# Norm scales computed in place: one product with the mean matrix, then logarithm and exponential

## The chip, the cores and the metric

The kernel runs on one core of a Trainium2 chip. The metric is the device time of one execution in microseconds (us). Before the change it is 3188.66 us, the median of three runs from 3187.61 to 3190.03.

The engines of the core work side by side, each through its own queue in order. In the profile PE is TensorE's products and PEld its weight loads, DVE is VectorE, ACT is ScalarE, POOL is GpSimd and SP the engine that issues most DMAs.

## What is computed

Four layers, one after the other, on a residual of 4 sequences of 1024 tokens with 128 channels, all in fp32. Each layer is a half FFN, an attention and a half FFN again, each behind a layer norm without weights:

```python
def _layernorm(x, axis=-1, eps=1e-05):
    m = jnp.mean(x, axis=axis, keepdims=True)
    v = jnp.var(x, axis=axis, keepdims=True)
    return (x - m) / jnp.sqrt(v + eps)
...
x = x + 0.5 * ffn(_layernorm(x))
x = x + attn(_layernorm(x))
x = x + 0.5 * ffn(_layernorm(x))
```

The FFN of layers 0 and 2 is a mixture of 8 experts (top 2, hidden size 512; gelu in layer 0, relu in layer 2). The FFN of layer 1 is dense with silu and hidden size 384. In layer 3 the FFN mixes each token with the one before it. Attention is: in layer 0, over the 16 heads within a token; in layer 1, softmax attention with rotary positions; in layer 2, a linear attention with decay; in layer 3, a recurrence over tokens, whose output goes through a norm over each head's 8 channels (a group norm) before it is gated and projected.

## The kernel before

**Layout.** The residual stays in SBUF, one tile of 128 channels x 1024 tokens for each sequence: channels lie on partitions and tokens along the free dimension. Work goes mostly in halves of 512 tokens, which fill one PSUM bank. A mean or a variance over channels is therefore a sum over partitions[...]. Constants for it are in the pack `c0`: `center` (identity minus 1/128, so that a product with it takes the mean off), `mean` (all 1/128), `ident` (identity). The pack `c3` has `gcenter` and `gmean` for the groups of layer 3.

**A norm.** It appears in five places with the same steps: `l1_ffn` (line 597, a whole sequence, from then on in two halves), `prepare` in `l1_attn` (line 671, a whole sequence), `l2_half` (line 861), `normed` (line 936, called by layer 3's FFN and by `l3_prepare`), and `l3_finish` (line 1133, the group norm). The steps, for four tiles of 128 tokens in a half:

1. one product with `center` into a bank; ScalarE squares it to SBUF, and a copy of it (`xc`) is made by ScalarE or VectorE;
2. for each tile of 128 tokens, a product with the squares as weights and one column of `mean` as moving operand; it gives the tokens' variances with tokens on partitions, one column for each tile;
3. ScalarE takes the root with the small constant added, VectorE the reciprocal, both on 4 or 8 columns (the function `scales`, line 262, does steps 2 and 3 for `l1_ffn`, `l2_half` and for layer 0's attention);
4. for each tile, a product of that column, broadcast to 128 columns as weights, with `ident`; it brings the scales back to tokens along the free dimension, the same on all partitions, in a bank;
5. VectorE multiplies `xc` by the bank.

In `l3_finish` step 2 has 16 columns of `gmean`, and between 3 and 4 ScalarE copies the 16 scales of each token to 128 columns (`wide`).

The routers of layers 0 and 2 and layer 0's attention have norms of their own kind, with tokens on partitions.

**Order.** The layers' tasks are Python generators. `lanes` (line 1197) interleaves several of them by the costs that each `yield` states; in layer 0 the dense FFNs of layer 1 stand beside the last experts, in layer 2 they stand at the start, and the attention halves stand beside experts; in layer 3 five lanes run: the recurrence, two with the starts and two with the ends of a sequence. A scheduler then orders each engine's instructions, and puts in the waits. In layer 1's attention TensorE's order is as written by hand: its main loop has steps of scores and values, and `prepare` for the next sequence advances by one `yield` with each step.

Nearly all products are issued by the helper `mm`, so that they carry its line, 227, in the profile. An fp32 product is two passes, and so two instructions of PE and of PEld. Where a function of ScalarE isn't in the table set that is loaded, the build puts a table load (ACT_TABLE_LOAD) ahead of it.

Of the kernel before, what the change touches and what calls it, by code (L numbers as in the profile page):

```python
# [12 lines left out]
AF = mybir.ActivationFunctionType  # L13
# [3 lines left out]
P = 128  # L17
# [42 lines left out]
def _constants():  # L60

    p = np.arange(P)
    f = np.float32
    n8, n16 = np.arange(8), np.arange(16)
    t = np.arange(P)

    c0 = [
        ("ident", np.eye(P, dtype=f)),
        ("mean", np.full((P, P), 1.0 / P, f)),
        ("rev", np.broadcast_to((8 - n8).astype(f), (P, 8))),  # L70
        ("below", (p[:, None] < p[None, :]).astype(f)),
        ("ones", np.ones((P, P), f)),
        ("lane", np.broadcast_to(p.astype(f), (P, P))),
        ("column", np.broadcast_to(np.arange(BLOCKS, dtype=f), (P, BLOCKS))),
        ("full", np.broadcast_to((SLOTS * np.arange(GT)).astype(f), (P, GT))),
        ("center", np.eye(P, dtype=f) - f(1.0 / P)),
        ("token", (1.0 + p[:, None] + P * np.arange(2 * GT)).astype(f)),
        *[
            (f"spare{g}", (1.0 + 2 * g * NT * P + p[:, None] + P * np.arange(blocks_of(g * NT))).astype(f))
            for g in range(1, GROUP + 1)  # L80
        ],
    ]

    dd = p % HD
    freqs = np.power(f(10000.0), -np.arange(0, HD, 2, dtype=f) / f(HD)).astype(f)
    angles = (np.arange(S, dtype=f)[:, None] * freqs).astype(f)
    sin, cos = np.sin(angles).astype(f), np.cos(angles).astype(f)
    sign = np.where(dd < HD // 2, -1.0, 1.0).astype(f)
    c1 = [
        ("cos", cos.T[dd // 2]),  # L90
        ("sin", sin.T[dd // 2] * sign[:, None]),
    ]

    n = np.maximum(t[None, :] - p[:, None], 0)
    bits = ((n[:, None, :] >> np.arange(7)[:, None]) & 1).astype(f)
    c2 = [("bit", bits), ("nobit", 1 - bits), ("causal", (t[None, :] >= p[:, None]).astype(f))]

    h, turned = p // HD, np.arange(2)[None, :, None]
    c3 = [
        ("sums", (h[:, None, None] == np.arange(32) - NH * turned).astype(f)),  # L100
        ("vrows", ((p % 32)[:, None, None] == NH * turned + h).astype(f)),
        ("bonus", (h[:, None] == p % NH).astype(f)),
        ("gcenter", np.eye(P, dtype=f) - (p[:, None] % NH == p % NH).astype(f) / HD),
        ("gmean", (p[:, None] % NH == n16).astype(f) / HD),
    ]
    return {"c0": c0, "c1": c1, "c2": c2, "c3": c3}

# [98 lines left out]
class Macaron:  # L206
# [55 lines left out]
    def scales(self, pool, wp, sq, tag, tiles=NT):  # L262

        var = self.t(pool, [P, tiles], "bank")
        for i in range(tiles):
            self.mm(var[:, i : i + 1], sq[:, i * P : (i + 1) * P], self.c0["mean"][:, 0:1])
        std = self.t(wp, [P, tiles], tag + "std")
        self.nc.scalar.activation(std, var, AF.Sqrt, bias=self.eps_ln)
        r = self.t(wp, [P, tiles], tag + "rstd")
        self.nc.vector.reciprocal(r, std)  # L270
        return r

# [322 lines left out]
    def l1_ffn(self, ps, wp, m, b):  # L597
        nc, c0 = self.nc, self.c0
        X = self.X[b]
        bank = lambda shape=(P, HALF): self.t(ps, list(shape), "bank")  # L600
        halves = [slice(h * HALF, (h + 1) * HALF) for h in range(2)]
        sq, xc = self.t(wp, [P, S], "sq", bufs=1), self.t(wp, [P, S], "xc", bufs=1)
        for c in halves:
            cen = bank()
            self.mm(cen, c0["center"], X[:, c])
            nc.scalar.activation(sq[:, c], cen, AF.Square)
            nc.vector.tensor_copy(xc[:, c], cen)
        r = self.scales(ps, wp, sq, "f")
        yield 4
        for hf, c in enumerate(halves):  # L610
            bc = bank((P, 4, P))
            for j in range(4):
                i = 4 * hf + j
                self.mm(bc[:, j, :], r[:, i : i + 1].to_broadcast([P, P]), c0["ident"])
            xn = self.t(wp, [P, HALF], "xn")
            nc.vector.tensor_tensor(xn, xc[:, c], bc.rearrange("p i t -> p (i t)"), ALU.mult)
            h = self.t(wp, [P, HIDC, HALF], "h", bufs=1)
            for i in range(HIDC):
                g = bank()
                self.mm(g, m["wg"][:, i, :], xn)  # L620
                s = self.t(wp, [P, HALF], "s")
                nc.scalar.activation(s, g, AF.Silu)
                u = bank()
                self.mm(u, m["wu"][:, i, :], xn)
                nc.vector.tensor_tensor(h[:, i, :], s, u, ALU.mult)
                yield 2
            o = bank()
            for i in range(HIDC):
                self.mm(o, m["wd"][:, i, :], h[:, i, :], start=i == 0, stop=i == HIDC - 1)
            self.add_half(b, c, o)  # L630
            yield 3
# [6 lines left out]
    def l1_attn(self, m, c1):  # L638
# [5 lines left out]
        with ExitStack() as ctx:  # L644
# [26 lines left out]
            def prepare(b):  # L671
# [5 lines left out]
                nc.scalar.copy(xc, cen)  # L677
                yield
                yield
                var = two((P, NT))  # L680
                for i in range(NT):
                    self.mm(var[:, i : i + 1], sq[:, i * P : (i + 1) * P], c["mean"][:, 0:1])
                std, r = self.t(self.lnp, [P, NT], "std"), self.t(self.lnp, [P, NT], "rstd")
                nc.scalar.activation(std, var, AF.Sqrt, bias=self.eps_ln)
                v.reciprocal(r, std)
                yield
                yield
                bc = two()
                for i in range(NT):
                    self.mm(bc[:, i * P : (i + 1) * P], r[:, i : i + 1].to_broadcast([P, P]), c["ident"])  # L690
                xn = self.t(self.lnp, [P, S], "xn")
                v.tensor_tensor(xn, xc, bc, ALU.mult)
                yield
                yield
                for w, wt, tag in ((m["wq"], m["wqt"], "qd"), (m["wk"], m["wkt"], "kd")):
# [165 lines left out]
    def l2_half(self, ps, wp, m, grow, X):  # L861
# [8 lines left out]
        q, qs = one("q", (P, 4, P)), one("qs", (P, 4, P))  # L870
        nc.scalar.activation(sq, cen, AF.Square)
        v.tensor_copy(xc, cen)
        r = self.scales(ps, wp, sq, "l", 4)
        bc = bank((P, 4, P))
        for j in range(4):
            self.mm(bc[:, j, :], r[:, j : j + 1].to_broadcast([P, P]), c0["ident"])
        v.tensor_tensor(xn, xc, bc.rearrange("p i t -> p (i t)"), ALU.mult)
        qp = bank()
        self.mm(qp, m["wq"], xn)
        nc.scalar.activation(q.rearrange("p c t -> p (c t)"), qp, AF.Relu, bias=m["bq"])  # L880
# [55 lines left out]
    def normed(self, ps, tmp, wp, b, h, before):  # L936

        nc, c0 = self.nc, self.c0
        x = self.X[b][:, h * HALF : (h + 1) * HALF]
        cen = self.t(ps, [P, HALF], "bank")  # L940
        self.mm(cen, c0["center"], x)
        sq, xc = self.t(tmp, [P, HALF], "n_sq"), self.t(tmp, [P, HALF], "n_xc")
        nc.scalar.activation(sq, cen, AF.Square)
        nc.scalar.copy(xc, cen)
        var = self.t(ps, [P, 4], "bank")
        for i in range(4):
            self.mm(var[:, i : i + 1], sq[:, i * P : (i + 1) * P], c0["mean"][:, 0:1])
        std, r = self.t(tmp, [P, 4], "n_std"), self.t(tmp, [P, 4], "n_r")
        nc.scalar.activation(std, var, AF.Sqrt, bias=self.eps_ln)
        nc.vector.reciprocal(r, std)  # L950
        bc = self.t(ps, [P, 4, P], "bank")
        for i in range(4):
            self.mm(bc[:, i, :], r[:, i : i + 1].to_broadcast([P, P]), c0["ident"])
        xn = self.t(wp, [P, HALF + 1], "xn", bufs=3)
        if before is None:
            nc.vector.memset(xn[:, 0:1], 0.0)
        else:
            nc.scalar.copy(xn[:, 0:1], before[:, HALF:])
        nc.vector.tensor_tensor(xn[:, 1:], xc, bc.rearrange("p i t -> p (i t)"), ALU.mult)
        return xn  # L960


# [170 lines left out]
    def l3_finish(self, ps, wp, m, c3, b, h, given):  # L1133
# [7 lines left out]
        sq, yc = self.t(wp, [P, HALF], "t1", bufs=1), self.t(wp, [P, HALF], "t2", bufs=1)  # L1141
        act(sq, cen, AF.Square)
        nc.scalar.copy(yc, cen)
        var = bank((P, 4, NH))
        for i in range(4):
            self.mm(var[:, i, :], sq[:, i * P : (i + 1) * P], c3["gmean"])
        std, rs = self.t(wp, [P, 4, NH], "gstd"), self.t(wp, [P, 4, NH], "grs")
        act(std, var, AF.Sqrt, bias=self.eps_gn)
        v.reciprocal(rs, std)
        wide = self.t(wp, [P, 4, HD, NH], "t3", bufs=1)  # L1150
        nc.scalar.copy(wide, rs.unsqueeze(2).to_broadcast([P, 4, HD, NH]))
        yield 5
        bc = bank((P, 4, P))
        for i in range(4):
            self.mm(bc[:, i, :], wide[:, i].rearrange("p j h -> p (j h)"), self.c0["ident"])
        v.tensor_tensor(yc, yc, bc.rearrange("p i t -> p (i t)"), ALU.mult)
        v.tensor_tensor(yc, yc, g, ALU.mult)
        o = bank()
        self.mm(o, m["olnb"], g, stop=False)
# [221 lines left out]
```

## Time and profile before

| | |
|---|---|
| median of the runs | 3188.66 us |
| the profiled execution | 3191.45 us |
| its span, first to last instruction | 3189.6 us |
| mean granted TensorE clock | 0.905 of full |
| instructions | 48448 |
| table loads, all of 1283 ns | 196 |
| LDWEIGHTS and MATMUL of `n_sq` (step 2 of `normed`) | 192 each |
| LDWEIGHTS and MATMUL of `n_r` (step 4 of `normed`) | 192 each |

A row of the page's groups has line, engine, operation, output and input with shapes, the count, busy time in us and the mean of one in ns, and then the idle time ahead of it with what ended it. In a timeline a row has start and duration in us. The chain that ended last is followed back from the last instruction to whatever released each step; its shares say which engine's work sets the end. The granted clock is the share of TensorE's full clock that the throttle let through.

### The profile page before, as it was taken

The numbers are of one execution on the slowest core, as the hardware profiler recorded it, in microseconds if no ns is written. First come the engines' busy times: TensorE is split into PE (matmuls) and PEld (weight loads), VectorE is DVE, ScalarE is ACT, GpSimd is POOL, SyncE is SP. The second block draws the span as 40 slices with busy tenths as digits, with TensorE's granted clock in tenths as the row PEclk, the third lists the DMA queues.
The fourth block names the chain that finished last, engine by engine and source line by source line (L and its number), as shares of the span: only waits on it lengthen the run. The fifth ranks groups of instructions, "written<-read, shape, count | busy, mean of one in ns | idle before, by whom it ended". The sixth has DMA issues, their size and how long they took to land.

```text
span 3189.6 us, 48448 instructions
## 1 busy us (share of the span) xinstructions
PE 2823.6 (89%) x18206; PEld 1677.6 (53%) x18206; DVE 1828.0 (57%) x3160; ACT 1633.3 (51%) x3633; POOL 794.8 (25%) x748
## 2 busy tenths in 40 slices
PE   7977548878969999999999999999998987899997
PEld 6856437666633333333333333579787985334333
DVE  3486967774226676676677774352565532355764
ACT  4655425656712565566556566455453544445342
POOL 3556306552440000000000000027543464000110
PEclk9988758888977999999999999989998997888997
DMA  6656315563500000000000000039555675000000
GB/s 218 217 169 203 115 51 169 166 196 105 159 15 9 6 6 5 6 5 6 20 5 6 3 1 1 9 115 297 191 182 164 205 260 167 0 0 0 7 7 13
DMA packets 122889, 277.63 MB, mean 87 GB/s; under 512 B 18016, under 2 KB 67296, under 8 KB 122528
## 3 DMA queue, kind: packets, MB, share of 16 engines
q1 hardware_dynamic: 101792, 231.77, 23.1%
q0 software_dynamic: 20864, 42.77, 4.5%
q8 instruction: 144, 2.36, 0.3%
q14 instruction: 89, 0.73, 0.1%
HBM read 238.43 MB, written 31.85 MB: 85 GB/s over the span
## 4 chain that ended last, share of the span: by engine, by line
PE 70%; DVE 8%; ACT 5%; DMA 3%; issue 2%; POOL 1%; ACTq 0%; SPq 0%; POOLq 0%; DVEq 0%
PE bank L227 36%; PE two L227 17%; PE o L227 8%; PE s L227 4%; DVE nm L729 2%; PE wave L1019 1%; ACT e_h L459 1%; DMA c_y<-res 1%; ACT L459 1%; DVE prod L554 1%; PE bank L449 1%; DMA e_xg<-rows,g_source 1%; DVE st L1117 1%; DVE o L556 1%; PE acc L1019 1%
## 5 line engine op out<-in xcount | busy, mean ns | idle before, releaser
L729 DVE TENSOR_REDUCE nm<-two 128x2 f32<-128x1024 f32 x512 | 626.8, 1225 | 287.8 <-PE s L227 268.4
L752 ACT ACTIVATE e<-s 128x512 f32<-128x512 f32 x1024 | 555.9, 594 | 405.7 <-PE s L227 402.7
L459 ACT ACTIVATE e_h<-bank,e_w 128x128 f32<-128x128 f32 x1304 | 449.5, 368 | 412.7 <-PE bank L227 378.3
L227 PE MATMUL s<-qm,kz 32*128 32x512 f32 x2048 | 633.7, 642 | 0.8 <-ACT e L752 0.8
L227 PE MATMUL bank<-e_x,e_w 128*128 128x128 f32 x2608 | 538.3, 309 | 85.9 <-ACT e_h L459 50.5
L227 PE MATMUL two<-kz,qz 32*128 32x512 f32 x2048 | 592.1, 663 | 21.5 <-DVE nm L729 2.7
L445 POOL DMA_INDIRECT e_xg<-rows,g_source x326 | 336.8, 1033 | 798.6 <-DVE g_target L412 353.5
L227 PEld LDWEIGHTS bank<-e_x,e_w 128*128 128x128 f32 x2608 | 410.0, 203 | 164.9 <-ACT e_h L459 94.0
L227 PE MATMUL bank<-e_w,e_h 128*128 128x128 f32 x2608 | 462.4, 293 | 18.4 <-ACT e_h L459 10.3
L471 POOL DMA_INDIRECT res<-e_y,g_target x326 | 358.9, 1101 | 282.4 <-DVE e_y L470 135.9
L227 PEld LDWEIGHTS bank<-e_w,e_h 128*128 128x128 f32 x2608 | 380.7, 202 | 40.1 <-ACT e_h L459 22.6
L227 PE MATMUL o<-e,va 128*32 128x256 f32 x4096 | 328.3, 392 | 0.1
L227 PEld LDWEIGHTS o<-e,va 128*32 128x32 f32 x4096 | 81.0, 108 | 389.6 <-issue 370.3
L227 PEld LDWEIGHTS two<-kz,qz 32*128 32x128 f32 x2048 | 159.4, 188 | 239.7 <-issue 163.6
L227 PEld LDWEIGHTS s<-qm,kz 32*128 32x128 f32 x2048 | 206.7, 183 | 11.4 <-issue 7.8
L470 DVE TENSOR_TENSOR e_y<-bank,e_w 128x128 f32<-128x128 f32 x326 | 93.9, 288 | 202.8 <-PE bank L227 189.3
L451 DVE COPY e_x<-bank 128x128 f32<-128x128 f32 x326 | 92.8, 285 | 189.7 <-PE bank L449 178.5
L717 POOL COPY va<-vd 128x256 f32<-128x256 f32 x16 | 6.7, 432 | 626.6 <-PE o L227 538.2
L1124 POOL TENSOR_TENSOR z<-st,r 128x512 f32<-128x512 f32 x32 | 46.2, 1443 | 416.8 <-DVE st L1117 333.3
L449 PE MATMUL bank<-c,e_xg 128*128 128x128 f32 x326 | 96.8, 298 | 34.0 <-DMA e_xg<-rows,g_source 31.0
L227 PE MATMUL bank<-g_cols,g_lanes 128*128 128x39 f32 (+1 forms) x512 | 83.4, 325 | 26.8 <-DVE g_cols L392 25.9
L227 PEld LDWEIGHTS bank<-g_cols,g_lanes 128*128 128x128 f32 x512 | 83.3, 251 | 30.3 <-issue 28.6
(300 smaller groups left out, 3683.2 us busy)
## 6 DMA issues: line engine op xcount, KB each, us to landing
e_w<-in_l0m_dram SPq DMA_DIRECT2D x170, 578.0 KB
e_w<-in_l2m_dram SPq DMA_DIRECT2D x156, 578.0 KB
c_y<-res SPq DMA_DIRECT2D x32, 512.0 KB
rows<-g_xt SPq DMA_DIRECT2D x16, 512.0 KB
e_xg<-rows,g_source POOLq DMA_INDIRECT x326
res<-e_y,g_target POOLq DMA_INDIRECT x326
x<-in_x_dram SPq DMA_DIRECT2D x4, 512.0 KB
qz<-qd SPq DMA_DIRECT2D x64, 32.0 KB
```

The costliest lines, as they stand in the source:

```text
L227: self.nc.tensor.matmul(out, lhsT, rhs, start=start, stop=stop)
L445: nc.gpsimd.indirect_dma_start(out=xg, out_offset=None, in_=rows[:, :], in_offset=at(source[:, k : k + 1]))
L449: nc.tensor.transpose(tp, xg, self.c0["ident"])
L451: nc.vector.tensor_copy(x, tp)
L459: nc.scalar.activation(h[:, fc, :], o[:, fc, :], func, bias=w[:, 2 * FC * P + fc : 2 * FC * P + fc + 1])
L470: nc.vector.tensor_tensor(y, o, w[:, MOE_W - D :], ALU.add)
L471: ins = nc.gpsimd.indirect_dma_start(out=res[:, :], out_offset=at(target[:, k : k + 1]), in_=y, in_offset=None)
L554: v.tensor_tensor(pv, ex.unsqueeze(2).to_broadcast(sh), values.unsqueeze(1).to_broadcast(sh), ALU.mult)
L729: v.tensor_reduce(nm[:, it, h, 2 * pair : 2 * pair + 2], s, AX.X, ALU.max, negate=True)
L752: nc.scalar.activation(es[g], s, AF.Exp, scale=scale)
L1019: i = self.nc.tensor.matmul(out, lhsT, rhs, start=start, stop=stop).ins
L1124: (pool if i else v).tensor_tensor(z, st[:, 0:HALF], r, ALU.mult)
```

## The change

Steps 2 to 4 are replaced in all five places. One product of the whole `mean` matrix (128 x 128) with the squares gives the variance of each token on all partitions at once, with tokens along the free dimension; for the groups, `gmean` is widened from 16 to 128 columns. ScalarE then computes the inverse root there, as exp(-0.5 ln(var + eps)), in two activations of the full width, the second over its own output in SBUF. VectorE's multiplication reads the result from SBUF instead of a bank.

```diff
-        ("gmean", (p[:, None] % NH == n16).astype(f) / HD),
+        ("gmean", (p[:, None] % NH == p % NH).astype(f) / HD),
...
+    def spread_scales(self, ps, sq, eps, mean=None):
+        var = self.t(ps, [P, HALF], "bank")
+        self.mm(var, self.c0["mean"] if mean is None else mean, sq)
+        self.nc.scalar.activation(sq, var, AF.Ln, bias=eps)
+        self.nc.scalar.activation(sq, sq, AF.Exp, scale=-0.5)
+        return sq
...
 l1_ffn
-        r = self.scales(ps, wp, sq, "f")
+        for c in halves:
+            self.spread_scales(ps, sq[:, c], self.eps_ln)
         yield 4
-        for hf, c in enumerate(halves):
-            bc = bank((P, 4, P))
-            for j in range(4):
-                i = 4 * hf + j
-                self.mm(bc[:, j, :], r[:, i : i + 1].to_broadcast([P, P]), c0["ident"])
+        for c in halves:
             xn = self.t(wp, [P, HALF], "xn")
-            nc.vector.tensor_tensor(xn, xc[:, c], bc.rearrange("p i t -> p (i t)"), ALU.mult)
+            nc.vector.tensor_tensor(xn, xc[:, c], sq[:, c], ALU.mult)
...
 prepare
-                var = two((P, NT))
-                for i in range(NT):
-                    self.mm(var[:, i : i + 1], sq[:, i * P : (i + 1) * P], c["mean"][:, 0:1])
-                std, r = self.t(self.lnp, [P, NT], "std"), self.t(self.lnp, [P, NT], "rstd")
-                nc.scalar.activation(std, var, AF.Sqrt, bias=self.eps_ln)
-                v.reciprocal(r, std)
+                nc.scalar.activation(sq, project(c["mean"], sq), AF.Ln, bias=self.eps_ln)
+                nc.scalar.activation(sq, sq, AF.Exp, scale=-0.5)
                 yield
                 yield
-                bc = two()
-                for i in range(NT):
-                    self.mm(bc[:, i * P : (i + 1) * P], r[:, i : i + 1].to_broadcast([P, P]), c["ident"])
                 xn = self.t(self.lnp, [P, S], "xn")
-                v.tensor_tensor(xn, xc, bc, ALU.mult)
+                v.tensor_tensor(xn, xc, sq, ALU.mult)
...
 l2_half
-        r = self.scales(ps, wp, sq, "l", 4)
-        bc = bank((P, 4, P))
-        for j in range(4):
-            self.mm(bc[:, j, :], r[:, j : j + 1].to_broadcast([P, P]), c0["ident"])
-        v.tensor_tensor(xn, xc, bc.rearrange("p i t -> p (i t)"), ALU.mult)
+        v.tensor_tensor(xn, xc, self.spread_scales(ps, sq, self.eps_ln), ALU.mult)
...
 normed
-        var = self.t(ps, [P, 4], "bank")
-        for i in range(4):
-            self.mm(var[:, i : i + 1], sq[:, i * P : (i + 1) * P], c0["mean"][:, 0:1])
-        std, r = self.t(tmp, [P, 4], "n_std"), self.t(tmp, [P, 4], "n_r")
-        nc.scalar.activation(std, var, AF.Sqrt, bias=self.eps_ln)
-        nc.vector.reciprocal(r, std)
-        bc = self.t(ps, [P, 4, P], "bank")
-        for i in range(4):
-            self.mm(bc[:, i, :], r[:, i : i + 1].to_broadcast([P, P]), c0["ident"])
+        self.spread_scales(ps, sq, self.eps_ln)
...
 l3_finish
-        var = bank((P, 4, NH))
-        for i in range(4):
-            self.mm(var[:, i, :], sq[:, i * P : (i + 1) * P], c3["gmean"])
-        std, rs = self.t(wp, [P, 4, NH], "gstd"), self.t(wp, [P, 4, NH], "grs")
-        act(std, var, AF.Sqrt, bias=self.eps_gn)
-        v.reciprocal(rs, std)
-        wide = self.t(wp, [P, 4, HD, NH], "t3", bufs=1)
-        nc.scalar.copy(wide, rs.unsqueeze(2).to_broadcast([P, 4, HD, NH]))
+        self.spread_scales(ps, sq, self.eps_gn, c3["gmean"])
         yield 5
-        bc = bank((P, 4, P))
-        for i in range(4):
-            self.mm(bc[:, i, :], wide[:, i].rearrange("p j h -> p (j h)"), self.c0["ident"])
-        v.tensor_tensor(yc, yc, bc.rearrange("p i t -> p (i t)"), ALU.mult)
+        v.tensor_tensor(yc, yc, sq, ALU.mult)
```

More of the change, by code (lines that the diff above doesn't have):

```diff
@@ L63, in _constants @@
     f = np.float32
-    n8, n16 = np.arange(8), np.arange(16)
+    n8 = np.arange(8)
     t = np.arange(P)
@@ L958, in normed @@
             nc.scalar.copy(xn[:, 0:1], before[:, HALF:])
-        nc.vector.tensor_tensor(xn[:, 1:], xc, bc.rearrange("p i t -> p (i t)"), ALU.mult)
+        nc.vector.tensor_tensor(xn[:, 1:], xc, sq, ALU.mult)
         return xn
```

## The prediction

> **What bounds the kernel now.** I read the page's engine shares first, then its chain that ended last, then busy time by stretch, and last the chain and the timeline inside a norm.
>
> ```profile
> PE 2823.6 (89%) x18206; PEld 1677.6 (53%) x18206; DVE 1828.0 (57%) x3160; ACT 1633.3 (51%) x3633; POOL 794.8 (25%) x748
> ...
> PE 70%; DVE 8%; ACT 5%; DMA 3%; issue 2%; POOL 1%; ACTq 0%; SPq 0%; POOLq 0%; DVEq 0%
> ```
>
> The chain that sets the end is TensorE's for 70% of the span, ScalarE's for 5%, although ScalarE is busy half the time. So a microsecond taken from TensorE is mostly a microsecond gained, and one added to ScalarE mostly isn't, until ScalarE's answers come later than TensorE's other work covers. By stretch (start:end, length, busy us of PE, PEld, DVE, ACT, POOL, granted clock, DMA share, GB/s):
>
> ```profile
> 0.00:715.00 715.00, 515.78 (x3096) 441.47 (x3097) 483.81 (x902) 378.45 (x972) 333.91 (x292) 0.83 0.53 167
> 715.00:915.00 200.00, 174.12 (x879) 123.60 (x878) 67.73 (x187) 125.17 (x240) 52.75 (x55) 0.89 0.37 113
> 915.00:2010.00 1095.00, 1053.62 (x8767) 378.77 (x8765) 702.61 (x686) 598.30 (x1088) 52.51 (x58) 0.97 0.03 6
> 2010.00:2260.00 250.00, 237.19 (x1342) 186.45 (x1341) 99.55 (x275) 120.80 (x344) 98.02 (x97) 0.92 0.49 159
> 2260.00:2490.00 230.00, 215.97 (x1492) 193.21 (x1492) 137.44 (x434) 105.04 (x305) 96.09 (x99) 0.93 0.54 172
> 2490.00:2690.00 200.00, 174.91 (x1301) 160.50 (x1299) 80.64 (x275) 100.87 (x322) 115.31 (x117) 0.94 0.73 236
> 2690.00:3190.00 500.00, 451.98 (x1336) 193.56 (x1336) 256.20 (x404) 204.71 (x364) 46.18 (x32) 0.85 0.01 5
> ```
>
> These are layer 0 up to its first dense FFN, its dense FFNs, layer 1's attention, layer 2 in three parts, layer 3. TensorE is at 87 to 96% wherever a changed norm runs. The first changed norm starts at about 717 us, so a quarter of the span can't move. Now one norm of layer 3 in the chain (start, us, what), where nothing lies beside it:
>
> ```profile
> 3149.41 0.61 ACT n_sq L943
> 3150.06 1.07 PE bank L227 x8
> 3151.15 0.27 ACT n_std L949
> 3151.44 0.19 DVE n_r L950
> 3151.68 1.17 PE bank L227 x8
> 3152.87 0.70 DVE xn L959
> ```
>
> From the end of the square to the multiplication: 2.85 us, of which TensorE works 2.24. The table load for the root isn't there: another root had left its table in place.
>
> **What the skill says.** "ScalarE: Activation LUTs", section "What ACT_TABLE_LOAD costs": about 1283 ns for a load plus about 1380 ns of drain at each change of set. The trace has the 1283 in every load, but no drain: at 3136.37 a load starts 0.02 us after the copy before it ends, and the root starts 0.02 us after the load. I use 1.28. The same page, "Table sets: the hidden batching unit", says that a logarithm followed by an exponential needs one load, there being a set with both. The changed kernel, built, stands otherwise: in its order of instructions a load precedes nearly every logarithm and another its exponential. The order decides. "TensorE: Matmul & The Clock Gate", section on the clock gate: idle stretches put TensorE at half clock. The trace agrees: a product of 512 columns shows 1.02 us at 3129.82 and after, and 1.92 us in the first lines below.
>
> **The change, part by part.** It was 32 half-sequence norms in layer 3 (24 `normed`, 8 group norms), 8 halves of `l2_half`, 16 halves of `l1_ffn`, and 4 whole-sequence norms in `prepare`.
>
> *Off TensorE.* Per half: 4 variance products with the squares as weights and 4 spreading products, each product two passes, so 8 and 8 instructions; on: one product of 512 columns, 2 passes. Occupancy at full clock: 0.97 and 0.97 us (weight loads of eight passes at 3150.05 and 3151.68) against 0.86 (2 x 0.43, the spacing of consecutive 512-column passes). Saved: 1.08 us. At half clock:
>
> ```profile
> 2697.66 1.86 PE L227 MATMUL bank<-c,n_sq 128*128 128x1 f32 x8 [0.69 <-ACT n_sq L943]
> ...
> 2700.18 2.04 PE L227 MATMUL bank<-c,n_r 128*128 128x128 f32 x8 [0.66 <-DVE n_r L950]
> ...
> 2702.02 1.92 PE L227 MATMUL bank<-x,c 128*128 128x512 f32 x2
> ```
>
> 1.78 + 1.78 - 1.71 = 1.85. With a half-clock share of (1 - clock)/0.5: layer 3 1.31 us x 32 = 42; layer 2 1.19 x 16 = 19; layer 0 1.25 x 8 = 10; `prepare` about 2.2 us each, three of them inside a full TensorE stream, 6.5. Sum 77 us. The built order agrees in count: 448 products fewer, 896 of 18206 rows.
>
> *On ScalarE.* Counting loads in the built orders: 196 before, 259 after: +9 in layer 0, 0 in layer 1 (there the root's load becomes the logarithm's), +28 in layer 2, +26 in layer 3. 63 x 1.28 = 81 us. Rows for the two functions:
>
> ```profile
> L883 ACT ACTIVATE k<-bank,l2a 128x512 f32<-128x512 f32 x8 | 5.5, 688 | 1.4 <-PE bank L227 1.4
> ...
> L994 ACT ACTIVATE t<-t 128x512 f32<-128x512 f32 x16 | 10.1, 629 | 0.5
> ```
>
> Logarithm 0.69 (from a bank, with a bias column), exponential 0.63 (from SBUF): 1.32 x 56 = 74; the four wide ones about 1.1 + 1.06 each, 9. Minus the roots (52 at 0.26 to 0.31, 14) and the wide copies (4.9). Sum +144 us, 51% to about 56%. VectorE loses only reciprocals of 0.2 to 0.5 us (12 us in all, under cover); its multiplication reads SBUF for PSUM at the same 0.69 (row of `qs`, 0.692).
>
> *The new wait.* From the end of the variance product to the normalised tile: 0.69 + 1.28 + 0.63 + 0.69 and four hand-offs of 0.03 to 0.05 = 3.45 us, all without TensorE. Behind it in ScalarE's order stand gelus, silus, tanhs and evictions of banks; TensorE, in order, waits for those. Before, the wait was in two pieces of about 0.6 and 0.75 us with products between. What hides it is TensorE's work placed between product and first use, read off the built order at full clock:
>
> - Layer 3: 19 of 24 norms have 3.4 us or more; five have 1.72, 2.58, 1.72, 0.86 and 0. Exposed there 10.4 us; the same places lost about 5.5 before: +5. The group norms' old path is as long as the new one (the last: variance products end at 3163.98, multiplication at 3168.04, with load, root, reciprocal, wide copy and products between, 4.06 us): 0. Further, 62 of ScalarE's 144 us lie here, on an engine 41% busy; bounds 0 and 31 (half of it late for TensorE), I take a quarter, +15. Layer 3: -42 + 5 + 15 = -22.
> - Layer 2, attention halves: 2.64 us of cover, with relus of the experts in the queue between and behind. 1.2 to 2 us exposed each, 1.5 x 8 = 12, against -9.5: +3.
> - Layer 2's dense FFNs: the first two sequences' four halves each take load, logarithm, load, exponential in turn (4 x 3.9 us) before the first silu; before, that silu came at 2022.08. It comes some 9 us later; two or three us of TensorE's work fill that. +7 and a little, against -9.5: about -1.
> - Layer 0's dense FFNs: -10, and 21 us more on a ScalarE that is 63% busy between gelus; half of it late: 0.
> - Layer 1: the load count is the same; the logarithm holds its bank for 0.85 us more than the root did, but TensorE waited for another bank then anyway (it stood from 1520.1 to 1521.0). -6.5 + 1.5 = -5.
>
> One bank fewer per norm is taken; that can only help. The queues of SP and POOL keep their instructions, with a few scatters and gathers in another place: 0, bounds -5 and +5.
>
> Sum: -22 + 3 - 1 + 0 - 5 = -25 us. The profiled execution took 3191.45 us (span 3189.6), 2.8 above the median of 3188.66; off the median that gives **3164 us**.
>
> **Rivals.**
>
> *A, the forecast:* TensorE's saving, a third kept. 0.48.
>
> *B, slower: table changes become the path.* Place: ScalarE's queue in layer 2 and 3, where each norm now holds it for 3.9 us (two loads, two functions) instead of 0.3 to 1.5, with expert activations and evictions behind. Price 144 us; it decides when over 77/144 = 54% of that is late for TensorE. At two thirds: -77 + 96 = +19, 3208 us. For: 63 more loads that a static order may not have made room for. Against: before, ScalarE's share of the chain was 5% of the span, a tenth of its busy time. 0.25.
>
> *C, all hidden:* -77, 3112 us. For: covers over 3.4 us in most places of layer 3. Against: layer 2's covers. 0.13.
>
> *D, nothing comes of it:* TensorE's shorter work is paid back as waits and, since it idles in longer pieces, as half clock; 3188 us. For: layer 3's clock is already 0.85 at 90% busy, and a single 3.45 us pause in place of two short ones can tip it. 0.14.
>
> **How the numbers follow.** A measurement of this kernel can tell about 0.2%, 6.4 us, from no change. A's own range is 3140 to 3180 (its 15 and 12 at their bounds). For 8 in 10 the range must go half into C and into B: 3125 to 3207. Faster: A 0.46, C 0.13, D 0.04: 0.63. Within: A 0.01, D 0.08, B 0.02: 0.11. Slower: the rest of B and D, A 0.01: 0.26.
>
> **What would show it.** Rows of PE 17310 and busy time down by some 70 us; ACT busy near 1777 us, 259 loads of 1283 ns; layer 3 shorter by about 20 us, layer 1 by 5, layer 2 and layer 0's end about even; in the tail a gap of about 3.4 us on TensorE between the variance product and the next. I am wrong if waits of PE for ACT's e_h or for evictions grow by more than 50 us in layers 2 and 3 (B), if layer 3's clock falls under 0.82 (D), or if no such gap appears anywhere (C).

## The result, and the profile after

The changed kernel takes 3216.22 us (median of 6 runs, 3209.14 to 3225.12), the kernel before, run beside it, 3189.09. The ratio is 1.009, 95% interval 1.0071 to 1.0108: 27 to 29 us slower, where 25 faster was forecast. The profiled execution has a span of 3207.2 us, against 3189.6; it is the fastest of the six, so the views below account for 17.6 us of the loss and not for all of the median's 27. First the engine shares of the kernel after:

```profile
PE 2764.0 (86%) x17310; PEld 1559.3 (49%) x17310; DVE 1822.5 (57%) x3108; ACT 1767.3 (55%) x3756; POOL 800.5 (25%) x748
```

TensorE's rows fell to 17310 and its busy time by 59.6 us; ScalarE's rose by 134.0. Both were foreseen. By stretch, the kernel after (columns as in the prediction's table; the cuts are at this run's own first changed norm, start of layer 1, and so on):

```profile
711.50:913.00 201.50, 165.52 (x761) 108.82 (x761) 67.01 (x183) 144.02 (x260) 54.60 (x56) 0.90 0.37 111
913.00:2008.00 1095.00, 1049.46 (x8647) 366.15 (x8646) 700.41 (x680) 605.27 (x1091) 51.45 (x57) 0.97 0.04 6
2008.00:2275.50 267.50, 236.01 (x1244) 175.87 (x1245) 102.17 (x280) 146.10 (x376) 99.53 (x99) 0.90 0.47 154
2275.50:2505.00 229.50, 204.02 (x1333) 176.59 (x1332) 129.57 (x407) 121.66 (x308) 91.83 (x94) 0.93 0.53 162
2505.00:2722.80 217.80, 185.15 (x1350) 165.22 (x1348) 87.06 (x300) 110.95 (x344) 118.15 (x119) 0.94 0.71 223
2722.80:3207.20 484.40, 412.63 (x878) 128.57 (x878) 251.63 (x355) 261.32 (x406) 48.97 (x32) 0.86 0.01 5
```

The same cuts in the kernel before, for layer 2's first part and layer 3:

```profile
2009.00:2262.00 253.00, 239.29 (x1352) 187.94 (x1352) 101.81 (x282) 122.93 (x351) 99.40 (x99) 0.92 0.49 160
2697.00:3189.60 492.60, 447.80 (x1326) 191.68 (x1326) 252.67 (x387) 202.26 (x356) 46.18 (x32) 0.86 0.01 5
```

Layer 3: TensorE's busy time fell from 447.8 to 412.6 us, but its idle time (length less busy) rose from 44.8 to 71.8. Layer 2's first part: busy 239.3 and 236.0, idle 13.7 and 31.5, at a clock of 0.90 for 0.92.

The table below cuts each profiled run at the first start of the same tiles (first square of the dense FFNs' norms, first square of `prepare`, last copy `os`, first and last square of `l2_half`, first `n_sq`, end), in us. The kernels of the experiments are in it too. "Start" is layer 0 before any changed norm; only before_joint and joint_all change something in it. Each row is one execution, and equal instructions vary: the other starts run from 712.8 to 721.9, layer 1 of mix and one_set takes 1081.3 and 1084.2, layer 3 of no_l1ffn and after 490.0 and 484.4. Differences of a few us in one cell prove little.

| run | start | layer 0, dense FFNs | layer 1 | layer 2, dense FFNs | attention | rest | layer 3 |
|---|---|---|---|---|---|---|---|
| before | 717.2 | 199.8 | 1091.4 | 255.3 | 217.1 | 216.2 | 492.6 |
| after | 712.8 | 201.9 | 1092.6 | 269.8 | 225.8 | 219.9 | 484.4 |
| one_set | 720.4 | 199.3 | 1084.2 | 254.3 | 212.6 | 218.7 | 460.0 |
| abs_rsqrt | 721.6 | 190.6 | 1086.8 | 253.4 | 212.3 | 218.6 | 465.9 |
| only_l3 | 717.6 | 200.9 | 1090.7 | 255.5 | 217.1 | 215.1 | 484.5 |
| no_l1ffn | 721.4 | 196.5 | 1095.2 | 256.2 | 225.7 | 217.7 | 490.0 |
| before_loads | 716.0 | 199.5 | 1093.7 | 251.3 | 220.8 | 216.3 | 512.2 |
| before_joint | 727.4 | 198.6 | 1087.0 | 252.8 | 217.9 | 217.2 | 485.1 |
| no_roots | 714.3 | 180.3 | 1087.1 | 253.7 | 213.1 | 217.4 | 462.6 |
| joint_all | 734.5 | 200.3 | 1081.2 | 256.7 | 212.4 | 216.3 | 460.8 |
| load_behind | 721.9 | 199.8 | 1086.9 | 264.6 | 227.8 | 220.5 | 475.3 |
| two_ahead | 719.6 | 202.1 | 1085.2 | 267.0 | 225.7 | 219.5 | 477.9 |
| mix | 720.9 | 189.7 | 1081.3 | 254.4 | 212.6 | 218.6 | 460.0 |

Before to after: -4 in the start, +2 and +1 in layer 0's dense FFNs and layer 1, +27 in layer 2, -8 in layer 3. The loss is made in layer 2, and layer 3's gain is a third of what was hoped.

What happens at layer 2's start is seen in stretches of 10 us, from the same point of the work (columns: stretch, length, busy us of PE, PEld, DVE, ACT, POOL, clock, DMA share, GB/s). Before:

```profile
2012.00:2022.00 10.00, 9.67 (x57) 6.87 (x56) 4.75 (x10) 5.30 (x8) 0.00 (x0) 1.00 0.20 64
2022.00:2032.00 10.00, 10.00 (x26) 4.39 (x25) 4.03 (x6) 3.58 (x6) 0.00 (x0) 1.00 0.00 0
```

and after:

```profile
2011.00:2021.00 10.00, 6.03 (x14) 2.32 (x12) 3.26 (x5) 8.39 (x10) 0.00 (x0) 0.88 0.20 64
2021.00:2031.00 10.00, 9.41 (x18) 3.59 (x17) 3.06 (x6) 9.85 (x12) 0.00 (x0) 0.77 0.00 0
...
2071.00:2081.00 10.00, 8.29 (x28) 4.13 (x27) 3.42 (x6) 9.70 (x23) 0.00 (x0) 1.00 0.00 1
```

ScalarE, 55% busy over the stage, is at 84 to 99% in these three (in the four left out it is at 34 to 62%), and TensorE idles 4 us in the first ten. The timeline of the kernel after shows what fills it (start, us, engine, instruction, and in brackets the engine's idle time before it and what ended it):

```profile
2013.40 1.28 ACT L278 ACT_TABLE_LOAD   x1 [1.30 <-PE bank L227]
...
2015.40 1.28 ACT L279 ACT_TABLE_LOAD   x1
2016.69 0.63 ACT L279 ACTIVATE sq<-sq 128x512 f32<-128x512 f32 x1
2017.34 1.28 ACT L278 ACT_TABLE_LOAD   x1
2018.63 0.69 ACT L278 ACTIVATE sq<-bank,eps_ln 128x512 f32<-128x512 f32 x1
2019.22 0.59 ACT L615 ACTIVATE sq<-bank 128x512 f32<-128x512 f32 x1
...
2019.86 2.08 PE L227 MATMUL bank<-sq,c 128*128 128x512 f32 x2 [3.97 <-ACT sq L615]
...
2029.49 0.60 ACT L628 ACTIVATE s<-bank 128x512 f32<-128x512 f32 x1
```

Loads for logarithm (L278) and exponential (L279) alternate; the second sequence's square stands behind three of them, and TensorE waits 3.97 us for it. The first silu starts at 2029.49. Before:

```profile
2022.08 0.60 ACT L622 ACTIVATE s<-bank 128x512 f32<-128x512 f32 x1 [0.82 <-PE bank L227]
```

Layer 2 begins at 2007.3 in the kernel after and at 2008.4 before (last copy `os`), so that the silu is 8.5 us late. The squares of the routings (L310 after) stand behind the next norms in the same queue, and the experts wait for the routings. SP's own queue, before and after:

```profile
2075.25 18.37 SPq L307 DMA_DIRECT2D rows<-g_xt  x2
2102.09 4.35 SPq L443 DMA_DIRECT2D e_w<-in_l2m_dram  x5
```

```profile
2085.23 14.38 SPq L316 DMA_DIRECT2D rows<-g_xt  x2
2112.90 3.81 SPq L452 DMA_DIRECT2D e_w<-in_l2m_dram  x5
```

Counted from the last copy `os`, the routed rows are written 11.1 us later and the first expert weights fetched 11.9 us later.

### The profile page after: what moved, and what is told of

It reads as the page before. It is cut to its first block, busy times and chain, and to the rows that moved or that the text cites. A ratio compares the mean times of both kernels' runs of the same rounds, so it can differ in the third digit from the quotient of the medians.

```text
span 3207.2 us, 46741 instructions
## 1 busy us (share of the span) xinstructions
PE 2764.0 (86%) x17310; PEld 1559.3 (49%) x17310; DVE 1822.5 (57%) x3108; ACT 1767.3 (55%) x3756; POOL 800.5 (25%) x748
## 5 line engine op out<-in xcount | busy, mean ns | idle before, releaser
L227 PE MATMUL bank<-e_x,e_w 128*128 128x128 f32 x2608 | 534.6, 308 | 100.0 <-ACT e_h L468 65.5
L227 PE MATMUL bank<-e_w,e_h 128*128 128x128 f32 x2608 | 457.6, 291 | 21.9 <-ACT e_h L468 13.7
L227 PEld LDWEIGHTS s<-qm,kz 32*128 32x128 f32 x2048 | 207.5, 183 | 13.8 <-issue 7.8
L479 DVE TENSOR_TENSOR e_y<-bank,e_w 128x128 f32<-128x128 f32 x326 | 93.8, 288 | 210.5 <-PE bank L227 198.6
```

Of the source, the lines that this page charges most:

```text
L227: self.nc.tensor.matmul(out, lhsT, rhs, start=start, stop=stop)
L479: nc.vector.tensor_tensor(y, o, w[:, MOE_W - D :], ALU.add)
```

## The experiments

Theories: **T1**, the 63 extra table changes on ScalarE cost the time. **T2**, the full-width functions and the long wait themselves. **T3**, the new static order of instructions. T4 to T6 came with the later runs.

**Loads taken out, nothing else moved (one_set).** After the instructions have been ordered, the load ahead of each logarithm is set by hand to the table set that holds both functions:

```diff
+    _one_set(nc)
...
+                if i.func == AF.Ln and not loaded:
+                    placed.append(mybir.InstLoadActFuncSet(
+                        name=nc.get_next_instruction_name(), engine=i.engine, debug=i.debug, ins=[], outs=[], act_func_set_id=6))
+                loaded = i.func == AF.Ln or (loaded and i.func == AF.Exp)
+            placed.append(i)
```

> The changed kernel with every order of instructions kept, but each logarithm's table load names the set that holds the exponential too, so the exponential needs none: 196 loads in place of 259 (layer 0 122, layer 1 1, layer 2 21, layer 3 52). T1 (the 63 extra table changes, standing in ScalarE's queue ahead of silus, routing and relus, are what cost the time): 3172 us, between 3160 and 3182; the first expert of layer 2 comes within 4 us of where it came before, instead of 12.6 later. T2 (the two full-width functions and the one long wait per norm are the cost; loads fall into idle time): 3210, between 3204 and 3216. T3 (the new static order, which puts routing and experts later, is the cost): as T2, and the first expert of layer 2 stays over 9 us late.

Measured: 3151.49 us, ratio to before 0.9879 (0.9859 to 0.9899). That beats both kernels, 38 us under before, and goes beyond T1's range. The first expert of layer 2 starts 123.5 us after layer 1's last `os` copy; before it was 124.7, after 137.0. T1 holds, and T3 can't carry these 65 us, since the order is the same. They are gone for 80.8 us of loads. In the profiled executions, which lie 58 apart: 30 in layer 2 (23 loads), 24 in layer 3 (30 loads), 8 in layer 1 (7 loads; the softmax's exponential is in the same set), 3 in layer 0's dense FFNs (3 loads), less 8 in the start, where nothing differs. Layer 3 of one_set:

```profile
2689.00:3149.50 460.50, 398.08 (x879) 125.20 (x878) 251.69 (x355) 222.67 (x376) 50.50 (x32) 0.89 0.01 5
```

TensorE idles 62.4 us there for 71.8 after, and is busy 398.1 us for 412.6 with the same products, at a clock of 0.89 for 0.86: of the 24 us, 9 are waits and 14 are products that ran at a slower clock (busy time times clock is 354 to 355 us in both).

**One function (abs_rsqrt).**

```diff
-        self.nc.scalar.activation(sq, var, AF.Ln, bias=eps)
-        self.nc.scalar.activation(sq, sq, AF.Exp, scale=-0.5)
+        self.nc.scalar.activation(sq, var, AF.Abs_reciprocal_sqrt, bias=eps)
```

`prepare` is changed likewise.

> The changed kernel with one full-width function, the inverse root of the absolute value, in place of logarithm and exponential: one load and 0.69 us of work per norm, 204 loads in all. T1: about as one_set, 3172, since nearly the same loads go. T2: half the functions' work goes and each norm's wait is 0.63 us (and a load) shorter, 3195. Both at once: about 3160.

3148.67 us, 0.987 (0.9851 to 0.989). It does without 39 us of exponentials (56 of 0.63 and 4 wide ones of 1.06) and has 8 loads, 10 us, more than one_set; the time is the same within 3 us. So T2's functions were not the main cost, though this kernel has an order of its own and the two aren't cleanly separated. In layer 0's dense FFNs it is 9 us shorter, in layer 3, with 4 loads more, 6 longer.

**Parts of the change (only_l3, no_l1ffn).** In only_l3, `l1_ffn`, `l2_half` and `prepare` are as before; in no_l1ffn only `l1_ffn` is:

```diff
-        for c in halves:
-            self.spread_scales(ps, sq[:, c], self.eps_ln)
+        r = self.scales(ps, wp, sq, "f")
...
-            nc.vector.tensor_tensor(xn, xc[:, c], sq[:, c], ALU.mult)
+            nc.vector.tensor_tensor(xn, xc[:, c], bc.rearrange("p i t -> p (i t)"), ALU.mult)
```

> Only layer 3's norms and group norms are changed; layers 0 to 2 are as before. If the stages add up as the two traces read (layer 3 8 us shorter, the rest 26 longer): 3181, between 3176 and 3186. If layer 3's gain was only room left by a late layer 2: 3189 or more.

> The changed kernel with the dense FFNs' norms as before. If the late start of layer 2's experts (14.5 us by its end) comes from these norms' loads and functions: 3199, between 3193 and 3204, first expert of layer 2 within 3 us of before. If it comes from what the attention halves do to the order: 3213 or more.

only_l3: 3187.66 us, 0.9988 (0.9979 to 0.9997), outside the first range and not in the second. The profiled execution has layer 3 at 484.5 as in the changed kernel, but lies 4 us under the median; the medians show a gain of some 4 us for that stage by itself, not the 8 of the table. no_l1ffn: 3204.61 us, 1.0033 (1.002 to 1.0046), just over its range. The first expert of layer 2 starts 124.8 us after the last `os` copy, as in the kernel before. Layer 2's first part is back (256.2), its attention isn't (225.7). So the dense FFNs' norms carry the first 14 us of layer 2's loss, the attention halves' the other 9.

**Loads put into the kernel before (before_loads).** Again loads are placed after the ordering, where a root's output is one of these norms':

```diff
+                if i.func == AF.Sqrt and re.sub(r"(_\d+)+$", "", i.outs[0].memref) in roots:
+                    for s in (3,) if loaded else (5, 3):
+                        placed.append(mybir.InstLoadActFuncSet(
...
+                            act_func_set_id=s))
```

> The kernel before with one more table load ahead of the root of each of the 52 norms that the change touches, and nothing else: 248 loads in place of 196 (layer 0 +4, layer 1 +4, layer 2 +12, layer 3 +32; 66.7 us of ScalarE). T1 (a load costs the path most of its length wherever a norm stands): at what one_set showed per load (layer 3 0.8 us, layer 2 1.3, layers 0 and 1 about 1) 26 + 16 + 8 = 50 us more, 3240, between 3222 and 3258. T4 (loads cost only in the changed kernel, whose single long wait has no products beside it; the kernel before hides them): 3205 or less.

3211.07 us, 1.0066 (1.0052 to 1.008): +21, 0.4 us for a load of 1.28, where one_set had won 1.0. T1 in the form "so much per load" falls, and so does T4. Layer 3 bears 20 of it for 32 loads, layer 2 nothing for 12. In layer 3 one can see where: summed over the 24 norms of `normed`, the time from the end of the variance products to the start of the root grew from 9.5 to 29.0 us, by as much as the stage. Where no load stood there before, an added one mostly lies beside the products; where one did, the second delays the root by its whole 1.28 us in 10 of 17 places. So a load has no fixed price; it may be free.

**The joint set without the spread product (before_joint).**

```diff
-        self.nc.scalar.activation(std, var, AF.Sqrt, bias=self.eps_ln)
+        self.nc.scalar.activation(std, var, AF.Ln, bias=self.eps_ln)
...
-        self.nc.vector.reciprocal(r, std)
+        self.nc.scalar.activation(r, std, AF.Exp, scale=-0.5)
```

The other norms are changed likewise, and `_one_set` places the loads.

> The kernel before, its products as they were, but the roots of the columns of variances as logarithm and exponential from one table set: 197 loads (layer 1 has 1 in place of 8, layer 0 has 7 more, layer 2 two more). T1: what one_set gains over the kernel before is the spread product's, not the set's; only layer 1's loads are won here, 8 us, less some in layer 0: 3182, between 3176 and 3190. T5 (one_set's gain is mostly the joint set's and the missing reciprocals'): 3165 or less.

3187.94 us, 0.9998 (0.9989 to 1.0008): no gain on the whole. T5 falls as it was put, but the table shows two parts: the start, where the function `scales` also serves layer 0's attention and 5 loads are added, is 10 us longer, and the rest is 14 us shorter (7 in layer 3, 4 in layer 1). one_set's stages behind the start are 43 us shorter. So most of what one_set wins is the spread product's, let through by the set; up to a third of it may be the set's and the missing reciprocals'.

**The floor (no_roots).**

```diff
-        self.nc.scalar.activation(sq, var, AF.Ln, bias=eps)
-        self.nc.scalar.activation(sq, sq, AF.Exp, scale=-0.5)
+        self.nc.scalar.activation(sq, var, AF.Identity, bias=eps, scale=0.0)
```

`prepare` is changed likewise.

> The changed kernel with one full-width function that every table set has (a constant in place of the inverse root, which is left out) where logarithm and exponential were: 141 loads. This is the floor of the change, with no table changes for norms at all. T1: one_set less 55 loads (layer 0 16, layer 2 8, layer 3 31) at 0.8 to 1.3 us: 3102, between 3090 and 3115. T2 (the long wait itself, not the loads, eats what one_set lost of TensorE's 80 us): 3135 or more.

3130.55 us, 0.9801 (0.9781 to 0.9821). Below T2's figure and above T1's range: 55 loads and 60 functions fewer than one_set bring 21 us, 19 of them, by the table, in layer 0's dense FFNs, where abs_rsqrt has 9 already. In layers 2 and 3 it is no shorter than one_set for 39 loads fewer. Layer 3:

```profile
2665.90:3128.50 462.60, 413.05 (x878) 128.47 (x878) 248.24 (x355) 165.11 (x313) 50.07 (x32) 0.86 0.01 5
```

TensorE idles 49.5 us here, 13 fewer than in one_set, but the same products take 15 us longer, at a clock of 0.86 for 0.89. With fewer loads and functions the waits are shorter, and the clock takes it back; less idle time in sum is not a faster clock. What sets the clock isn't shown (the order of instructions differs too). With the norms' inverse roots left out, in this order, the spread product gives some 60 us of TensorE's 80.

**All roots by the joint set (joint_all).** `scales` as in before_joint, `route` likewise, and each load takes the set that serves longest:

```diff
-            nc.scalar.activation(std, ssq, AF.Sqrt, bias=self.eps_ln, scale=1.0 / D)
-            v.reciprocal(r, std)
+            nc.scalar.activation(std, ssq, AF.Ln, bias=self.eps_ln, scale=1.0 / D)
+            nc.scalar.activation(r, std, AF.Exp, scale=-0.5)
...
+                    loaded = max(SERVED[i.func], key=lambda s: run(s, n))
```

> The changed kernel with the joint set, the roots of the routings and of layer 0's attention norms also as logarithm and exponential from it, and every load taking the set that serves longest: 188 loads (layer 0 127, layer 1 1, layer 2 14, layer 3 46). T1: against one_set, layer 2 wins 7 x 1.3, layer 3 6 x 0.8 and layer 0 loses 5 x 0.9: 3142, between 3134 and 3150. T2: 3150, as one_set.

3166.07 us, 0.9925 (0.9911 to 0.9939), outside both expectations and 15 us worse than one_set with fewer loads. The table places it: 734.5 in layer 0's start against 720.4, equal elsewhere. before_joint, which changed layer 0's attention norms alone there, shows 727.4. Whether the longer chain in each routing or the new order costs this wasn't separated.

**Where the load stands (load_behind, two_ahead).** Position and number of loads were still mixed, since a load between two dependent functions is exposed while one ahead of the logarithm lies beside the variance product. Layer 3's last norm in the kernel after shows both:

```profile
3189.23 2.07 PE L227 MATMUL bank<-n_sq,c 128*128 128x512 f32 x2 [0.69 <-ACT n_sq L938]
3189.67 1.28 ACT L278 ACT_TABLE_LOAD   x1
3191.34 0.69 ACT L278 ACTIVATE n_sq<-bank,eps_ln 128x512 f32<-128x512 f32 x1 [0.39 <-PE bank L227]
3192.05 1.28 ACT L279 ACT_TABLE_LOAD   x1
3193.34 0.63 ACT L279 ACTIVATE n_sq<-n_sq 128x512 f32<-128x512 f32 x1
3194.00 0.69 DVE L946 TENSOR_TENSOR xn<-n_xc,n_sq 128x512 f32<-128x512 f32 x1 [7.65 <-ACT n_sq L279]
...
3194.75 2.07 PE L227 MATMUL bank<-xn,now_k 128*128 128x512 f32 x2 [3.45 <-DVE xn L946]
```

The first load ends before the product does and costs nothing; the second is in TensorE's gap of 3.45 us. In one_set the same gap is 2.17:

```profile
3134.49 0.69 ACT L278 ACTIVATE n_sq<-bank,eps_ln 128x512 f32<-128x512 f32 x1 [1.69 <-PE bank L227]
3135.21 0.63 ACT L279 ACTIVATE n_sq<-n_sq 128x512 f32<-128x512 f32 x1
3135.87 0.69 DVE L946 TENSOR_TENSOR xn<-n_xc,n_sq 128x512 f32<-128x512 f32 x1 [6.37 <-ACT n_sq L279]
...
3136.62 2.08 PE L227 MATMUL bank<-xn,now_k 128*128 128x512 f32 x2 [2.17 <-DVE xn L946]
```

So two runs keep the number of loads and move the second: behind the exponential (the diff), or ahead of the logarithm with the first (`for s in (6,) if one else (5, 6)`).

```diff
+            if func == AF.Ln and not logs:
+                load(i, 6)
+            placed.append(i)
...
+                if not logs:
+                    load(i, 0)
```

> The changed kernel in its own order and with as many table loads (263 for 259), but each norm's second load stands behind its exponential instead of between logarithm and exponential (one load of the joint set ahead, then both functions, then a load of the exponential's own set). T1 (ScalarE's queue: what counts is how much it carries): 3212, between 3204 and 3222. T6 (the chain of the norm: a load costs where it stands between two functions that depend on each other, and is free where ScalarE would wait for the variance product or nothing waits for what is behind it): 3165, between 3153 and 3180; layer 3 within 6 us of one_set's 460.

> The same with both loads ahead of the logarithm (264 loads). T1: 3212 as well. T6: the first load lies beside the variance product (0.9 to 2.1 us) and the second lies partly beyond it, so layer 3 comes between one_set's 460 and the changed kernel's 484, and the whole to about 3185, between 3170 and 3200.

load_behind: 3198.7 us, 1.0033 (1.002 to 1.0046). two_ahead: 3200.86 us, 1.0042 (1.0029 to 1.0055). Position is worth 15 to 18 us (most of layer 1's loss, about a third of layer 3's, 3 to 5 us at layer 2's start), far less than T6 said; it also fits layer 3 of before_loads, where the added load stands between variance and root. The other three quarters go only with the loads, though T1's 3212 was too high as well. What fits them, argued and not shown by a run of its own, is ScalarE at its limit. Counting stretches of 5 us in layer 3 with ScalarE busy 4.5 us or more: before 3 of 98, after 17 of 96, load_behind 18 of 94, one_set 4 of 91, before_loads 4 of 102. With the grid started elsewhere the counts move (before 1 to 3, after 10 to 19, load_behind 15 to 19, one_set 3 to 9, before_loads 3 to 12), but at nearly every start after and load_behind stay above the other three. Part of the 15 us of layer 3 between load_behind and one_set is again the clock: the products are busy 410.0 and 398 us. The start of layer 2 in load_behind:

```profile
2012.50:2022.50 10.00, 6.00 (x14) 2.30 (x14) 3.86 (x7) 9.63 (x13) 0.00 (x0) 0.93 0.19 64
2022.50:2032.50 10.00, 10.00 (x18) 4.25 (x19) 2.66 (x6) 9.84 (x11) 0.00 (x0) 0.73 0.00 0
```

It is as full as in the changed kernel, and the first expert starts 134.1 us after the last `os` copy, hardly sooner. In one_set the same twenty microseconds read:

```profile
2007.70:2017.70 10.00, 10.00 (x23) 4.13 (x23) 5.64 (x11) 8.14 (x14) 0.00 (x0) 1.00 0.19 64
2017.70:2027.70 10.00, 10.00 (x24) 4.38 (x23) 4.63 (x8) 5.82 (x8) 0.00 (x0) 1.00 0.01 2
```

TensorE doesn't idle, and ScalarE is free again in the second ten.

**The best of both (mix).** one_set, with `l1_ffn`'s norms by the one function of abs_rsqrt.

> one_set, with the dense FFNs' norms (layers 0 and 2) by the one inverse-root function of abs_rsqrt; 193 loads. If the stages of the two runs add up (layer 0's dense FFNs 199 to 191, the others as in one_set): 3143, between 3137 and 3149. If what abs_rsqrt showed in layer 0 was the luck of one order: 3151.

3139.34 us, 0.984 (0.9826 to 0.9854): 48 us faster than before, the fastest kernel here that computes everything. The stages add up. The edit:

```diff
+        if one:
+            self.nc.scalar.activation(sq, var, AF.Abs_reciprocal_sqrt, bias=eps)
+            return sq
...
-            self.spread_scales(ps, sq[:, c], self.eps_ln)
+            self.spread_scales(ps, sq[:, c], self.eps_ln, one=True)
```

## Why the prediction was wrong

The steps that failed are the allowances for ScalarE's extra work, in layer 2 above all: the waiting was put too small, and the time off TensorE too large, in layer 2 where the clock fell with it. Stage by stage the profiled execution misses the forecast by 2.1 us in layer 0's dense FFNs, 6.2 in layer 1, 15.5, 5.7 and 3.7 in layer 2's three parts and 13.8 in layer 3, less 4.4 in the start, which no edit touches. That is 42.6, from -25 to the +17.6 of the two spans.

- **Layer 2, -1 for the dense FFNs and +3 for the attention halves.** Measured +14.5 and +8.7, and +3.7 in the rest, which had nothing put down. In the first part the forecast was +7 and a little of waiting against 9.5 off TensorE; idle time grew by 17.8 and busy time fell by 3.3, at a clock of 0.90 for 0.92. "It comes some 9 us later; two or three us of TensorE's work fill that" saw the first silu rightly (8.5 us), and stopped there. Behind it the same queue holds the next two sequences' norms and the routings, with a root's load of their own, and 11.9 us later start the experts' weights. Three ten-microsecond stretches show ScalarE at 84 to 99%; I had judged its room by stages of 200 us and by its 5% of the chain.
- **Layer 3, -42 + 5 + 15 = -22.** Measured -8: busy time fell by 35.2 us where 42 was put, and idle time grew by 27.0 where 20 was. Without the second loads (one_set) the stage is at -33, so that these cost 24, more than half of it in products at a slower clock.
- **Off TensorE, 77 us.** Near as a price: one_set, with as many loads as before, is busy 80.1 us less. The changed kernel shows 59.6. Busy time times mean clock is nearly the same in both (2764.0 at 0.903 and 2743.5 at 0.909 give 2496 and 2494 us), so the lower clock explains the difference. That is rival D's half clock, as a part, though its sign, layer 3 under 0.82, didn't come: that clock is 0.86 as before. D's reason, idle time in longer pieces, isn't shown.
- **On ScalarE, +144 us.** Near: +134.0. The rows of the loads (line, operation, count, busy us, mean ns):

```profile
L278 ACT ACT_TABLE_LOAD x49 | 62.9, 1283 | 4.3 <-PE bank L227 3.5
L279 ACT ACT_TABLE_LOAD x46 | 59.0, 1283 | 0.8
```

The Trainium skill ("ScalarE: Activation LUTs", section "Table sets: the hidden batching unit") has one load for a logarithm and its exponential. The build took two, 49 and 46 in these rows, and the measurement decides; with the set named by hand, one_set has 30 and 4 at these lines.
- **The new wait, 3.45 us.** Right in the tail (3194.75 less 3191.30).
- **Layer 1, -5.** Measured +1. The count of loads was right (8 and 8), but the one between the two functions stands in the norm's chain, where there was one load before. With it moved behind the exponential (load_behind) the stage is at -4.5, with seven loads gone (one_set) at -7.
- **Layer 0's dense FFNs, 0.** Measured +2.
- **The rivals.** B's place in layer 2 and its mechanism are what the runs show, and its 3208 lies 8 us under the median; in layer 3 the loads cost 24 us, but the stage still gained. Its point of decision, 54% of ScalarE's extra 144 us late, was passed: (77 + 27) / 144 = 72%. The sign I named for it was badly chosen: waits of the experts' first products for `e_h` grew only from 50.5 to 65.5 us (page of each kernel), since the delay sits at squares, silus and routings, and in the clock. What I held against it, ScalarE's small share of the chain before the change, says who sets the end now, not how little room there is at single places.
- **A reading.** The product at 3129.82 takes 1.12 us in the trace; the 1.02 given for it is that of products after it.

## What to carry to other kernels

Before moving work to an engine that is "half busy", cut its busy time into stretches as long as the work's own burst (here 10 us), at the places where the new work will stand. In these runs the loads cost most where such stretches were full (argued from counts), or where a load stood between two steps that depend on each other (shown by moving it); the same load of 1.28 us was worth 0.4 us in one kernel and 1.0 in another. Count table loads in the built order, and where two functions that follow each other share a set, name that set; here naming it turned a loss of 0.9% into a gain of 1.2%. An idea that loses isn't refuted until its removable cost has been taken off.

## What the runs showed of the hardware

A load of a set that is already in place costs as much as any other: in before_loads all loads show a mean of 1283 ns, the repeated ones among them. The inverse root of the absolute value on 128x512 from a bank takes 0.687 us, as the logarithm does. In layer 3 the same 878 or 879 rows of TensorE took 412.6 us busy in the changed kernel, 398.1 in one_set and 413.1 in no_roots, at a granted clock of 0.86, 0.89 and 0.86 and with 71.8, 62.4 and 49.5 us of idle time. So the clock can give or take as much as the waits do, and the sum of the waits doesn't tell which.
